# A PV product of 64 rows widened to 128 rows in a fused attention and routed-FFN kernel

## The chip, the cores and the metric

The kernel runs on one core of a Trainium2 chip (trn2). The metric is the device time of one execution in microseconds (us). A profiled execution shows what each engine did: PE (TensorE, matmul), PEld (TensorE's weight load), DVE (VectorE), ACT (ScalarE), POOL (GpSimd) and SP (SyncE, which here issues the DMAs). A matmul on PE contracts over the partitions ("rows") of its two operands: the stationary one is loaded first by a weight load, the moving one is streamed through, one column of the result after another.

## The reference

Two batches of 512 tokens with a hidden size of 512 go through an attention layer with 32 query heads and 8 key/value heads of size 128, then a layer norm, then a base FFN with eight sparsemax-routed LoRA experts, and a layer norm again. Only the attention's product with V is touched here.

```python
q = (x @ Wq).reshape(B, S, 32, 128).transpose(0, 2, 1, 3)
k = (x @ Wk).reshape(B, S, 8, 128).transpose(0, 2, 1, 3)      # each repeated for 4 heads
v = (x @ Wv).reshape(B, S, 8, 128).transpose(0, 2, 1, 3)      # each repeated for 4 heads
scores = where(causal, einsum("bhqd,bhkd->bhqk", q, k) * 128**-0.5, -inf)
out = einsum("bhqk,bhkd->bhqd", softmax(scores), v)
x = layernorm(x + out.reshape(B, S, 4096) @ Wo)
x = layernorm(x + base(x) + experts(x))
```

## The kernel before

Every float32 operand is split into two float16 tiles, a high half and a low half, and a product is made of three matmuls: high by high, high by low, low by high (`mm3`, line 225, whose matmuls all carry line 228).

The work is cut into 16 groups, each a pair of a key/value head `g` and a batch `b`, and every group into four units, `i` = 0 to 3, each of 128 query rows of all four heads. `unit_a` makes the scores on PE, masks them and takes their maximum on DVE (line 369), their exponential on ACT (line 374), and writes the probabilities as two float16 halves into the tile `phl` (high half on ACT, line 350; low half on DVE, lines 354 and 356). A DMA transpose, issued by SP (line 99), turns `phl` into `pt`, with the keys on the partitions. `unit_b`, one unit later, multiplies V with `pt` into the PSUM tile `pv` and evicts it as `o` (ACT line 232, DVE line 233). `unit_c`, two units later, multiplies `o` with Wo and adds the result to `acc`.

While the units of one group run, the projections of the next group are made, in the order K and Q0 (unit 0), Q1 (unit 1), V (unit 2), Q2 and Q3 (unit 3). V's projection ends in `end_v`: ACT writes V's high half into the tile `v2`, DVE its low half, and ACT (line 307) fills a third part of `v2` with the first 64 keys of each block of 128, twice over. One DMA transpose then turns the three parts, 12 blocks of 128 by 128, into the tile `vt`, which has two buffers.

The causal mask makes two cases of a unit's 128 query rows, since for the first 64 of them only the first 64 keys of the diagonal block count. For these 64 rows the diagonal block's probabilities sit in `pt` as one block of 128 rows: the high halves for the 64 keys in the upper 64 rows, and the low halves for the same keys in the lower 64. That is why V's high half for those keys is stored twice (`vd`): one product of 128 rows gives high by high and high by low. The third product, V's low half by the high halves of the probabilities, uses 64 rows of both operands.

In `unit_b` a unit has 3`i` full products of 512 columns for the blocks under the diagonal, then two products of 256 columns for the first half of the query rows (`vd`, and the one of 64 rows), then three of 256 columns for the second half: 5, 8, 11 and 14 matmuls for `i` = 0, 1, 2, 3. The one of 64 rows stands after `vd`'s and before the three of the second half, and all others have 128 rows.

A scheduler decides the order of instructions on each engine for most of the kernel. The first stage, which loads the weights of group 0 and takes their scales, and the last stage, the final group and the FFN of four token tiles, have an order written out by hand. In the first stage `end_v(0, 0, PK[5])` stands in line 750, between `x_max` and the parked projection of Q3. SP's queue is in order: a DMA whose data are late holds those behind it. Behind the first `vt` transpose stand four loads of weights of group 1 (`w1raw`), four loads of `acc`, and the first `pt` transposes.

Of the kernel before, what the change touches and what calls it, by code (L numbers as in the profile page):

```python
# [10 lines left out]
F16 = mybir.dt.float16  # L11
# [6 lines left out]
P = 128  # L18
R = P // 2
NB, S, HID = 2, 512, 512  # L20
NT = S // P
# [18 lines left out]
def kernel(  # L40
# [18 lines left out]
    nc = tc.nc  # L59
    const = ctx.enter_context(tc.tile_pool(name="const", bufs=1))  # L60
    sb = ctx.enter_context(tc.tile_pool(name="sb", bufs=1))
# [19 lines left out]
        )  # L81
    cmh = const.tile([P, 1], F32, tag="cmh", name="cmh")
    nc.gpsimd.memset(cmh, -0.5)
    ones = const.tile([P, P], F32, tag="ones", name="ones")
    nc.gpsimd.memset(ones, 1.0)

# [11 lines left out]
    def sync_transpose(dst, src):  # L98
        hist.append(nc.sync.dma_start_transpose(dst, src).ins)
# [125 lines left out]
    def mm3(dst, pairs, first=True, last=True):  # L225
        n = len(pairs)
        for j, (a, b) in enumerate(pairs):
            nc.tensor.matmul(dst, a, b, start=first and j == 0, stop=last and j == n - 1)  # L228

    def cut_psum(hi, lo, psrc, by):  # L230

        nc.scalar.activation(hi, psrc, AF.Copy, scale=by)  # L232
        return nc.vector.scalar_tensor_tensor(lo, psrc, by, hi, ALU.mult, ALU.subtract).ins  # L233

    KT, QT, VT, LM = {}, {}, {}, {}
# [15 lines left out]
    def cut(b, g, j):  # L251
        return CUT if g else CK[b][:, j : j + 1]
# [19 lines left out]
    def pj(name, tag="pj"):  # L272
        return ps.tile([P, S], F32, tag=tag, name=name, bufs={"pj": 2, "S": 4}.get(tag, 1))

    def mul_k(g, b, tag="pj"):
        pk = pj(f"pk{g}_{b}", tag)
        project(pk, g, b, 4)
        return pk

    def end_k(g, b, pk):  # L280
        k2 = sb.tile([P, 2, S], F16, tag="K", name=f"k{g}_{b}", bufs=2)
        cut_psum(k2[:, 0, :], k2[:, 1, :], pk, cut(b, g, 4))
        KT[(g, b)] = k2
# [6 lines left out]
    def end_q(g, b, h, pq):  # L290

        if h % 2 == 0:
            QT[(g, b, h // 2)] = sb.tile([P, 2, 2 * NT, 2, R], F16, tag="Q", name=f"q{g}_{b}_{h}", bufs=NQ)
        q2 = QT[(g, b, h // 2)][:, :, :, h % 2, :]
        return cut_psum(q2[:, 0], q2[:, 1], pq.rearrange("p (j q) -> p j q", q=R), cut(b, g, h))

    def mul_v(g, b, tag="pj"):
        pv = pj(f"pvp{g}_{b}", tag)
        project(pv, g, b, 5)
        return pv  # L300

    def end_v(g, b, pv):
        v2 = sb.tile([P, 3, S], F16, tag="V2", name=f"v2{g}_{b}")
        cut_psum(v2[:, 0, :], v2[:, 1, :], pv, cut(b, g, 5))

        keys = v2[:, 0, :].rearrange("p (t k) -> p t k", k=P)[:, :, :R]
        nc.scalar.copy(
            v2[:, 2, :].rearrange("p (t a k) -> p t a k", a=2, k=R), keys.unsqueeze(2).broadcast_to([P, NT, 2, R])
        )
        vt = sb.tile([P, 3 * NT, P], F16, tag="VT", name=f"vt{g}_{b}", bufs=2)  # L310
        sync_transpose(vt, v2.rearrange("p a s -> p (a s)"))
        VT[(g, b)] = vt

    def proj(g, b, j):
        if j == 4:
            factors(g, b)
            end_k(g, b, mul_k(g, b))
        elif j == 5:
            end_v(g, b, mul_v(g, b))
        else:  # L320
            end_q(g, b, j, mul_q(g, b, j))

# [66 lines left out]
    def unit_b(g, b, i):  # L389
        vt = VT[(g, b)]  # L390
        pt = PT.pop((g, b, i))
        pt = pt.rearrange("p e k (h q) -> p e k h q", q=R)
        pv = ps.tile([P, HPG, 2, R], F32, tag="PV", name=f"pv{g}_{b}_{i}")
        dst = pv.rearrange("p (e h) j q -> p j e h q", e=2)
        m = 2 * i + 1
        pairs = []
        for kt in range(i):
            ph, pl = (pt[:, :, k :: m][:, :, :2].rearrange("p e j h q -> p j e h q") for k in (kt, i + 1 + kt))
            vh, vl = vt[:, kt, :], vt[:, NT + kt, :]
            pairs += [(vh, ph), (vh, pl), (vl, ph)]  # L400
        if i:
            mm3(dst, pairs, last=False)

        vh, vl, vd = (vt[:, k * NT + i, :] for k in range(3))
        both = pt[:, :, i]
        mm3(dst[:, 0], [(vd, both), (vl[:R], both[:R])], i == 0, i == 0)
        ph, pl = pt[:, :, m + i], pt[:, :, m + 2 * i + 1]
        mm3(dst[:, 1], [(vh, ph), (vh, pl), (vl, ph)], i == 0)
        yield
        o2 = sb.tile([P, 2, HPG, 2, R], F16, tag="O", name=f"o{g}_{b}_{i}", bufs=2)  # L410
        cut_psum(o2[:, 0], o2[:, 1], pv, 2.0**-15)
        OT[(g, b, i)] = o2
        yield
# [269 lines left out]
    with tc.manual_schedule(engines={ET.PE, ET.DVE, ET.Activation, ET.Pool, ET.SP}):  # L683
        for c in range(KC):
            nc.sync.dma_start(x_raw[0][c], xt[0, :, c, :])
            if c == 0:
                load_w(4)
        for j in JS[1:]:
            load_w(j)
        for c in range(KC):  # L690
            nc.sync.dma_start(x_raw[1][c], xt[1, :, c, :])
        wo_raw = [load_raw(source(0, j), f"0_{j}", True) for j in ROWS]
        x0_raw = [load_raw(xt[0, :, c, :], f"x0_{c}") for c in range(KC)]
        w1_raw = [load_raw(source(1, j), f"1_{j}") for j in JS[:2]]
        load_x(0)

        sq0 = sb.tile([P, 8], F32, tag="sq", name="sq0", bufs=2)
        sq1 = sb.tile([P, 8], F32, tag="sq", name="sq1", bufs=2)
        PK[4] = pj("park4", "pj")
        for c in range(KC):  # L700
            x_hi(0, c)
            x_lo(0, c, nc.vector)
            if c < 2:
                n = slice(0, 1) if c == 0 else slice(1, KC)
                hi, lo = (a[:, n, :].rearrange("p c d -> p (c d)") for a in WR[4])
                raw = w_raw[4][:, n.start * P : n.stop * P]
                nc.scalar.copy(hi, raw)
                nc.vector.tensor_tensor(lo, raw, f(hi), ALU.subtract)
            project(PK[4], 0, 0, 4, [c])
        w_hi(0, nc.scalar.copy)  # L710
        w_lo(0, nc.vector)
        park(0, "pj")
        w_hi(1, nc.scalar.copy)
        w_lo(1, nc.gpsimd)
        park(1, "PV")
        w_hi(5, nc.scalar.copy)
        w_hi(2, nc.scalar.copy)
        w_lo(2, nc.gpsimd)
        w_hi(3, nc.scalar.copy)
        w_lo(3, nc.gpsimd)  # L720
        for c in range(KC):
            x_max(0, c)
        w_max(4)
        w_max(5)
        amax(mx[:, 6:7], mx[:, 9:13])
        for j in range(4):
            w_squares(sq0[:, j : j + 1], w_raw[j], "S")
        nc.scalar.activation(sq0[:, 4:7], mx[:, 4:7], AF.Square)
        w_lo(5, nc.vector)
        tot = total(sq0, 7, "0", "S")  # L730
        park(5, "wo")
        for c in (0, 1):
            x_hi(1, c)
            x_lo(1, c, nc.gpsimd)
        sc = sb.tile([P, 2, 8], F32, tag="sc0", name="sc0")
        SC[(0, False)] = sc
        scales(sc, tot, 7)
        x_factors(0, sc, 6)
        end_k(0, 0, PK[4])
        end_q(0, 0, 0, PK[0])  # L740
        factors(0, 0)
        end_q(0, 0, 1, PK[1])
        for c in (2, 3):
            x_hi(1, c)
            x_lo(1, c, nc.gpsimd)
        park(2, "S")
        for c in range(KC):
            x_max(1, c)
        amax(mx[:, 7:8], mx[:, 13:17])
        end_v(0, 0, PK[5])  # L750
        park(3, "S")
        for k in range(4):
            w_squares(mx[:, 17 + k : 18 + k], wo_raw[k], "S")
        amax(sq1[:, 1:2], mx[:, 17:21])
        nc.scalar.activation(sq1[:, 0:1], mx[:, 7:8], AF.Square)
        end_q(0, 0, 2, PK[2])
        tot = total(sq1, 2, "1")
        convert = split_x(0, x0_raw)
        next(convert)
        end_q(0, 0, 3, PK[3])  # L760
        sc1 = sb.tile([P, 2, 8], F32, tag="sc1", name="sc1")
        scales(sc1, tot, 2)
        SC[(0, True)] = sc1[:, :, 1:3]
        x_factors(1, sc1, 0)
        next(convert)

        w1 = sb.tile([P, KC, S], F32, tag="base0", name="w1raw")
        for n, j in enumerate(JS[2:]):
            w1_raw.append(w1[:, n, :])
            sync_load(w1[:, n, :].rearrange("p (c d) -> p c d", c=KC), source(1, j))  # L770
        load_x(1)
# [94 lines left out]
    for s in range(len(units) - NT):  # L866
        if s < len(units):
            g, b, i = units[s]
            k = s // NT
# [80 lines left out]
```

## Time and profile before

| | |
|---|---|
| time, median of 3 runs | 686.54 us (685.78 to 686.63) |
| the profiled execution's own time | 685.9 us |
| its span, first to last instruction | 684.1 us |
| PE busy | 669.8 us, 98% of the span |
| DVE busy | 534.1 us, 78% |
| ACT busy | 362.6 us, 53% |
| POOL busy | 244.2 us, 36% |
| granted PE clock, mean over the span | 0.997 |
| matmuls that write `pv` | 608, of which 64 have 64 rows |
| `vt` transposes | 16, median 1.62 us of SP each, 3.9 us to landing |
| `pt` transposes | 128, median 1.29 us of SP each, 3.6 us to landing |

A group in the profile is a set of instructions with one line, engine, operation and shape. Its "mean ns of one" is the time from an instruction's start to its end. Matmuls are pipelined, one starting before the last has ended, so what a matmul costs the engine is the distance from its start to the next one's start, which the timeline gives, and not its own duration. "128\*128 128x256" is a stationary operand of 128 rows by 128 columns and a moving one of 128 rows by 256 columns; "64\*128 64x256" has 64 rows in both.

### The profile page before, as it was taken

The page shows a single profiled execution, that of the slowest core. Times are in us where ns is not written, and L with a number is a line of the kernel's source. Part 1 is how long each engine was busy: PE and PEld are TensorE (multiplying, and loading weights), DVE is VectorE, ACT ScalarE, POOL GpSimd, SP SyncE. Part 2 cuts the span into 40 slices and gives each one's busy share as a digit, 9 for nine tenths or more (in the row PEclk, how much of TensorE's full clock was granted, in tenths as well). Part 3 has the DMA queues.
Part 4 walks back from the last instruction along what each step waited for, and adds up shares of the span by engine and source line. Part 5 has one row for each costly group of instructions (what it writes and reads, how often), then busy time and mean ns, then how long its engine had stood idle before and what let it go on. Part 6 is the DMA issues. An engine that isn't in the chain of part 4 may idle for free.

```text
span 684.1 us, 11487 instructions
## 1 busy us (share of the span) xinstructions
PE 669.8 (98%) x3596; PEld 344.7 (50%) x3596; DVE 534.1 (78%) x1701; ACT 362.6 (53%) x1030; POOL 244.2 (36%) x353
## 2 busy tenths in 40 slices
PE   8899999999999999999999999999999999999996
PEld 5665545445454545455454544454454545544453
DVE  6897877868697678778788787859777677878796
ACT  6875754566365554656355464626555464444520
POOL 4666450725617050645208067054406001100011
PEclk9999999999999999999999999999999999999998
DMA  8767391747447192555528355734625262453311
GB/s 326 238 104 154 90 208 38 156 109 176 72 73 151 29 216 39 128 118 126 128 54 214 76 103 107 179 64 79 145 42 110 40 118 48 87 112 73 70 44 46
DMA packets 197005, 76.80 MB, mean 112 GB/s; under 512 B 181712, under 2 KB 181712, under 8 KB 196944
## 3 DMA queue, kind: packets, MB, share of 16 engines
q1 hardware_dynamic: 196944, 76.07, 49.8%
q8 instruction: 28, 0.46, 0.3%
q14 instruction: 33, 0.27, 0.1%
HBM read 29.12 MB, written 2.10 MB: 46 GB/s over the span
## 4 chain that ended last, share of the span: by engine, by line
PE 87%; DVE 7%; ACT 2%; DMA 2%; issue 1%; POOL 0%; SPq 0%; POOLq 0%; ACTq 0%; DVEq 0%
PE pw L228 22%; PE pq L228 22%; PE pv L228 15%; PE s L228 12%; PE pvp L228 6%; PE pk L228 5%; PE pa L228 3%; PE park L228 1%; DVE phl L354 1%; ACT s L374 1%; DVE s L369 1%; DMA w1raw<-in_wq_dram 1%; DMA xraw<-in_xt_dram 1%; DVE mx L122 1%; DVE acc L434 1%
## 5 line engine op out<-in xcount | busy, mean ns | idle before, releaser
L374 ACT ACTIVATE s<-s,ast 128x192 f32<-128x192 f32 (+7 forms) x256 | 120.8, 472 | 159.9 <-DVE ast L369 156.2
L228 PE MATMUL pw<-w,o 128*128 128x512 f16 x768 | 177.0, 379 | 0.0
L228 PEld LDWEIGHTS <-w 128*128 128x128 f16 x1008 | 98.1, 98 | 110.5
L228 PE MATMUL pq<-xT,w 128*128 128x512 f16 x672 | 152.2, 379 | 0.0
L350 ACT ACTIVATE phl<-s,ast 128x192 f16<-128x192 f32 (+7 forms) x256 | 110.6, 512 | 23.1 <-DVE ast L343 21.0
L228 PE MATMUL pv<-pt,vt 128*128 128x512 f16 (+2 forms) x608 | 121.1, 325 | 0.3 <-DMA pt<-phl 0.3
L369 DVE CUSTOM_DVE_ANT_0 s<-s,mask,lm 128x192 f32<-128x192 f32 (+7 forms) x256 | 117.7, 519 | 0.7 <-PE s L228 0.7
L354 DVE SCALAR_TENSOR_TENSOR phl<-s,ast,phl 128x128 f16<-128x128 f32 (+2 forms) x224 | 112.4, 515 | 6.4 <-ACT phl L350 5.9
L228 PEld LDWEIGHTS <-o 128*128 128x128 f16 x768 | 74.8, 98 | 77.0 <-DVE o L233 0.7
L228 PE MATMUL s<-k,q 128*128 128x320 f16 (+7 forms) x768 | 106.3, 286 | 1.3 <-DVE phl L356 0.9
L228 PEld LDWEIGHTS <-vt 128*128 128x128 f16 (+1 forms) x608 | 53.8, 99 | 67.4 <-issue 21.3
L228 PEld LDWEIGHTS <-q 128*128 128x128 f16 x768 | 64.1, 98 | 43.1 <-issue 1.6
L260 POOL TENSOR_SCALAR lm<-sc,xs 128x1 f32<-128x1 f32 x15 | 4.0, 265 | 213.6 <-DVE sc L136 125.1
L119 POOL TENSOR_TENSOR w<-raw,w 128x512 f16<-128x512 f32 x70 | 79.5, 1155 | 0.3
L434 DVE SCALAR_TENSOR_TENSOR acc<-pw,lm,acc 128x512 f32<-128x512 f32 x64 | 47.8, 746 | 26.1 <-PE pw L228 25.7
L116 POOL TENSOR_SCALAR raw<-raw,sc 128x512 f32<-128x512 f32 x70 | 47.6, 690 | 56.6 <-issue 32.7
L233 DVE SCALAR_TENSOR_TENSOR o<-pv,o 128x512 f16<-128x512 f32 x64 | 43.7, 683 | 26.5 <-ACT o L232 26.5
L232 ACT ACTIVATE o<-pv 128x512 f16<-128x512 f32 x64 | 39.3, 613 | 42.8 <-PE pv L228 42.7
L122 DVE TENSOR_REDUCE mx<-raw 128x1 f32<-128x512 f32 x68 | 44.4, 678 | 14.9 <-DMA raw<-in_wo_dram 14.9
L374 ACT ACTIVATION_READ_ACCUMULATOR s<-s,ast 128x1 f32 x256 | 51.5, 201 | 0.0
L233 DVE SCALAR_TENSOR_TENSOR q<-pq,q 128x512 f16<-128x512 f32 x56 | 38.0, 683 | 15.8 <-ACT q L232 15.4
L232 ACT ACTIVATE q<-pq 128x512 f16<-128x512 f32 x56 | 34.0, 611 | 26.5 <-PE pq L228 26.5
(166 smaller groups left out, 643.0 us busy)
## 6 DMA issues: line engine op xcount, KB each, us to landing
raw<-in_wo_dram SPq DMA_DIRECT2D x32, 256.0 KB, 3.6
raw<-in_wq_dram SPq DMA_DIRECT2D x29, 256.0 KB, 4.2
xraw<-in_xt_dram SPq DMA_DIRECT2D x8, 256.0 KB, 4.9
raw<-in_wk_dram SPq DMA_DIRECT2D x8, 256.0 KB, 3.4
raw_x<-in_xt_dram SPq DMA_DIRECT2D x8, 256.0 KB, 4.6
acc<-in_x_dram SPq DMA_DIRECT2D x8, 256.0 KB, 5.5
pt<-phl SPq DMA_TRANSPOSE x128, 3.6
out_dram<-y SPq DMA_DIRECT2D x8, 256.0 KB, 2.0
```

Source lines behind the costliest of these rows:

```text
L116: nc.gpsimd.tensor_scalar(view, view, by, 1.0, ALU.mult, ALU.mult)
L119: return first.ins, nc.gpsimd.tensor_tensor(lo, view, hi, ALU.subtract).ins
L122: nc.vector.tensor_reduce(dst, view, AX.X, ALU.max, apply_absolute_value=True)
L228: nc.tensor.matmul(dst, a, b, start=first and j == 0, stop=last and j == n - 1)
L232: nc.scalar.activation(hi, psrc, AF.Copy, scale=by)
L233: return nc.vector.scalar_tensor_tensor(lo, psrc, by, hi, ALU.mult, ALU.subtract).ins
L260: engine.tensor_scalar(lm[:, 4:5], sc[:, 0, 4:5], XS[b][0], 1.0, ALU.mult, ALU.mult)
L350: nc.scalar.activation(hi, src[:, :n], AF.Copy, scale=by)
L354: nc.vector.scalar_tensor_tensor(lo, src[:, :m], by, hi[:, :m], ALU.mult, ALU.subtract)
L369: nc.vector.tensor_tensor_reduce(out=sc[:, :n], in0=sc[:, :n], in1=mask[:, S - n :], scale=lm[:, h // 2 : h // 2 + 1], scalar=BIG, op0=ALU ...
L374: nc.scalar.activation(sc[:, :n], sc[:, :n], AF.Exp, bias=st[:, 0, h : h + 1], scale=-1.0, accum_out=st[:, 1, h : h + 1])
L434: nc.vector.scalar_tensor_tensor(a, pw, LM[(g, b)][:, 7:8], a, ALU.mult, ALU.add)
```

## The change

The product of 64 rows becomes one of 128. `v2` gets a fourth part, one block of 128 keys for each block of the sequence: its first 64 keys are V's low half, its other 64 are zero. After the transpose this is the block `vz`, of 128 rows, and `both` is used whole: its lower 64 rows meet zeros. Since the zeros have to be written only once, `v2` is no longer taken from a pool for every group but is one tile that stays in place; GpSimd clears its fourth part at the start.

For every group ACT makes one more copy, of 4 by 64 elements per partition, and it reads what DVE writes as V's low half. The transpose has 16 blocks instead of 12, and `vt` 16 instead of 12. The copies and the transpose move into a function of their own, `turn_v`, which the ordinary groups call right after `end_v`. In the hand-written first stage it is called later than `end_v`: after `next(convert)`, which issues the split of two of the four tiles of x, and ahead of `end_q(0, 0, 3, ...)`.

```diff
     cmh = const.tile([P, 1], F32, tag="cmh", name="cmh")
     nc.gpsimd.memset(cmh, -0.5)
+    v2 = const.tile([P, 4, S], F16, tag="v2", name="v2")
+    nc.gpsimd.memset(v2[:, 3, :], 0.0)
...
     def end_v(g, b, pv):
-        v2 = sb.tile([P, 3, S], F16, tag="V2", name=f"v2{g}_{b}")
         cut_psum(v2[:, 0, :], v2[:, 1, :], pv, cut(b, g, 5))
 
-        keys = v2[:, 0, :].rearrange("p (t k) -> p t k", k=P)[:, :, :R]
+    def turn_v(g, b):
+
+        first, twice = (v2[:, k : k + 2, :].rearrange("p a (t k) -> p a t k", k=P) for k in (0, 2))
         nc.scalar.copy(
-            v2[:, 2, :].rearrange("p (t a k) -> p t a k", a=2, k=R), keys.unsqueeze(2).broadcast_to([P, NT, 2, R])
+            twice[:, 0].rearrange("p t (a k) -> p t a k", a=2), first[:, 0, :, :R].unsqueeze(2).broadcast_to([P, NT, 2, R])
         )
-        vt = sb.tile([P, 3 * NT, P], F16, tag="VT", name=f"vt{g}_{b}", bufs=2)
+        nc.scalar.copy(twice[:, 1, :, :R], first[:, 1, :, :R])
+        vt = sb.tile([P, 4 * NT, P], F16, tag="VT", name=f"vt{g}_{b}", bufs=2)
         sync_transpose(vt, v2.rearrange("p a s -> p (a s)"))
         VT[(g, b)] = vt
...
             end_v(g, b, mul_v(g, b))
+            turn_v(g, b)
...
-        vh, vl, vd = (vt[:, k * NT + i, :] for k in range(3))
+        vh, vl, vd, vz = (vt[:, k * NT + i, :] for k in range(4))
         both = pt[:, :, i]
-        mm3(dst[:, 0], [(vd, both), (vl[:R], both[:R])], i == 0, i == 0)
+        mm3(dst[:, 0], [(vd, both), (vz, both)], i == 0, i == 0)
...
         convert = split_x(0, x0_raw)
         next(convert)
+        turn_v(0, 0)
         end_q(0, 0, 3, PK[3])
```

## The prediction

> **What bounds the kernel now.** I read the busy shares and the chain of waits first.
>
> ```profile
> PE 669.8 (98%) x3596; PEld 344.7 (50%) x3596; DVE 534.1 (78%) x1701; ACT 362.6 (53%) x1030; POOL 244.2 (36%) x353
> ...
> PE 87%; DVE 7%; ACT 2%; DMA 2%; issue 1%; POOL 0%; SPq 0%; POOLq 0%; ACTq 0%; DVEq 0%
> ```
>
> PE is busy for 98% of the span and is 87% of the chain that ends last. By stages (the windows view), PE is busy 100.00 us of every 100 from 100 to 500 us. The idle time is in the first 45 us and after 598 us. In between, whatever shortens PE's stream shortens the kernel, if the other engines keep up. A busy PE can still hide stalls between overlapping matmuls, so I go to the timeline, for the smallest PV unit (`i` = 0, 5 matmuls) and the scores ahead of it:
>
> ```profile
> 303.57 1.31 PE L228 MATMUL s<-k,q 128*128 128x192 f16 x12
> 304.72 2.75 PE L228 MATMUL pq<-xT,w 128*128 128x512 f16 x12
> ...
> 307.31 0.27 PE L228 MATMUL pv<-pt,vt 128*128 128x256 f16 x1
> ...
> 307.51 0.28 PE L228 MATMUL pv<-pt,vt 64*128 64x256 f16 x1
> ...
> 307.73 0.50 PE L228 MATMUL pv<-pt,vt 128*128 128x256 f16 x3
> 308.06 0.28 PE L127 MATMUL totl<-fsq,ones 128*128 128x1 f32 x2
> ```
>
> Columns are start, length, engine, operation. Go from start to start. Six score matmuls of 192 columns and six of 256 take 304.72 - 303.57 = 1.15 us for 2,688 columns, so 256 columns cost 0.11 us; the three after 307.73 also take 0.33, 0.11 each. But the matmul before the one of 64 rows holds PE for 0.20 us, and the one of 64 rows for 0.22: 0.42 where two of 128 rows would take 0.22. The loss is **0.20 us per unit**. The longer units agree:
>
> ```profile
> 249.27 2.05 PE pv L228 x11
> ...
> 257.01 2.59 PE pq L228 x12
> 259.60 2.70 PE pv L228 x14
> ```
>
> Twelve of 512 columns take 2.59, 0.216 each. Fourteen PV matmuls are nine of these and five of 0.109: 2.49, against 2.70. Eleven are six and five: 1.84, against 2.05. The excess is 0.21 both times. The weight loads say why:
>
> ```profile
> L228 PEld LDWEIGHTS <-vt 128*128 128x128 f16 x544 | 47.8, 99 | 47.6 <-issue 1.8
> L228 PEld LDWEIGHTS <-vt 64*128 64x128 f16 x64 | 5.9, 93 | 19.8 <-issue 19.6
> ```
>
> The 64 small loads sit 19.6 us, 0.31 each, waiting for nothing that is visible, while the 544 full ones have 1.8 in all: the small load isn't pulled under the running matmul.
>
> **The matmul, rule against row.** The Trainium skill, "TensorE: Matmul & The Clock Gate", section "LDWEIGHTS (loading the stationary operand)", says a load's time goes by its columns and a 32-row load takes as long as a 128-row one. By that rule the change gains nothing, and the durations seem to agree: 93 against 99 ns for the loads, 280 against 275 ns for the matmuls. The same skill's "TensorEngine Tiling", section "Key Properties", says a change of tiling mode drains the array, and 64 by 128 is listed there as a mode of its own. Two changes per unit at the drain that the first page gives under "Step-by-step: what each phase is for" (about 128 cycles, 53 ns at 2.4 GHz) would be an estimate of 0.11 us per unit. The trace has 0.20, and the trace decides: the sum for 59 units is 0, 6.3 or 11.8 us by the three. After the change every matmul of the unit has the shape of its neighbours, whose distance is 0.11.
>
> How many of the 64 lie on the path? In the chain in order of time PE carries it without a break from 45 us to 598.36, when it goes to ACT and DVE (`o`, the routing of a token tile, scores). From there to 648.9 its longer pieces touch PE only at 610.5 and 623.7 to 627.8, in other matmuls. The units at 614, 622, 634, 644 and 658 us are off it, the one at 650.2 is on it. So 58 + 1 units: 59 x 0.199 (0.42 - 0.22, unrounded) = **11.7 us**; all 64 would be 12.7, the upper end.
>
> **ACT's second copy.** The copy it joins (512 elements) takes 0.64 us. The exponent-to-half cuts of line 350 take 0.695 at 512 and 0.493 at 256 elements, so half the size saves about 0.20: 0.44 us, 16 times, 7 us of an engine that is busy 53%. It also waits for DVE's low half, with the exponentials of the next unit queued behind it. In the groups from 85 us on the present copy ends within 0.44 us of the low half's end (161.53 against 161.63 us, for instance). Behind it:
>
> ```profile
> 160.92 0.61 ACT L307 COPY v<-v 128x512 f16<-128x512 f16 x1
> 164.61 0.61 ACT L374 ACTIVATE s<-s,ast 128x448 f32<-128x448 f32 x1 [3.07 <-DVE ast L369]
> ```
>
> ACT then idles 3.07 us for DVE's maximum; the groups to 560 us have 2.3 to 3.1. (In the second group, at 42.6, the low half is 1.9 behind and ACT has no idle time; there the new order puts the second copy behind four exponentials, at the low half's end.) Wait and copy are at most 0.9, so they cost nothing. Without that cover, the exponentials, `phl` and `pt` of unit 3 would be late.
>
> **The transpose.** 16 blocks for 12: SP's 1.62 us becomes at most 4/3 of it, 2.2, and 3.9 to landing at most 5.2 (estimates in proportion). Landings of `vt` come 21 to 27 us before the first PV in all groups but the first, so its own lateness is nothing. What follows in SP's queue is `pt` of unit 2 or 3 and weight loads; their `pt` lands 1.2 us or more before its PV from 64 us on. 0 to 0.5 us late costs nothing.
>
> **`v2` in place.** V's next high half is written long after the transpose has landed (at 41.3 us against about 32.5 in the first group, some 30 us later in the others), and the same wait existed with one pool buffer. Clearing the fourth part is one POOL fill at 2.3 us, where POOL has nothing until 9.45. Nothing.
>
> **The first group.** Here `turn_v` moves past four squares, Q2's cut and two x splits on ACT, and the transpose with it on SP:
>
> ```profile
> 24.63 1.54 SPq L99 DMA_TRANSPOSE vt<-v  x1
> 26.27 0.82 SPq L96 DMA_DIRECT2D w1raw<-in_wq_dram  x1
> ...
> 29.44 1.80 SPq L96 DMA_DIRECT2D acc<-in_x_dram  x4
> 32.68 1.19 SPq L99 DMA_TRANSPOSE pt<-phl  x1
> ```
>
> On ACT the squares come 0.6 earlier, but then wait for DVE's maximum as now (23.91); the splits end at 25.94, the two copies at about 26.9. The transpose issues there, 2.3 later than now, so `w1raw`, `acc` and the first `pt` follow 2.3 to 2.9 later: `pt` at about 34, 1 to 1.4 late, since SP had 1.4 us in hand. Q3's cut and what is behind it on ACT slips 0.9. Against this stands what the scheduler's new order shows: DVE no longer waits 0.91 us for `w1raw` ahead of K's cut, for which PE now idles 0.82, and seven more V-projection matmuls (1.6 us) are put ahead of the first PV on PE. `vt` lands near 32.5, PV starts at 37.4. Bounds: 0.8 gained to 2.4 lost. I take 0, near the middle of the two listed effects; both ends stay in the range.
>
> **Sum.** 685.9 of the profiled execution less 11.7 is 674.2 (span 684.1 to 672.4). The median of the runs is 0.64 above that execution: 686.54 - 11.7 = **674.8 us**.
>
> **Rivals.**
> 1. *The others can't follow (half the gain).* DVE is busy 77 to 79 of 100 us in the middle; with PE 1.8% shorter that is 79 to 81. `pt` has its least margin in the unit at 482 us (1.2) and 493 (1.5), against 0.2 us taken per unit; DVE's work is fed by PE's scores and moves with them. For it: three units after 440 us have under 1.6. If half is lost: 680.7.
> 2. *Nothing changes.* If the stall belongs to reading that block of `vt` or `pt`, and not to the 64 rows, it stays: 686.5. Against it: `vd` reads the same `pt` block just ahead without a late load.
> 3. *Slower, through ACT's wait.* Place: the second copy waits in ACT's order for V's low half; should DVE put that half late, unit 3's exponentials stand behind it in 14 groups. Cover is 1.9 us (2.3 idle less 0.44) and unit 3's `pt` margin, 3.05 in the mean (1.3 to 5.0). The change ends slower than before once the wait is over 1.9 + 3.05 + 11.7/14 = 5.8 us per group. At 7: 674.8 + 14 x (7 - 4.95) = 703.5. The trace has 0.44 or less in steady groups, 3.3 once in the first.
>
> **Chances.** Forecast, with at least three quarters of the gain: 0.86. Half: 0.08. Nothing: 0.03. Slower: 0.03. Differences under 0.2% (1.4 us) can't be told from none here. Faster 0.94, same 0.03, slower 0.03. The range goes from 686.5 - 12.7 - 0.8 = 673.0 up to the loss of a fourth of the gain, 677.8, which also holds the first group's worst case (677.2).
>
> **What would show it.** Right: no `64*128` shape; five matmuls of unit 0 in about 0.55 us instead of 0.75; PV of 14 in 2.50; the `issue` idle of `vt`'s loads near 1.8 us in all; the steady period of a group, from one V projection to the next, shorter by 0.8 us (four units). First group: the first PV at 37 to 39 us. Tail, from the last group's first PV to the end, unchanged within 1 us. Wrong: starts still 0.2 apart at `vz`, PE idle for `pt` behind ACT copies that wait on DVE, or a first PV past 40 us.

## The result, and the profile after

The changed kernel takes 677.42 us (677.06 to 678.01, 4 runs) against 686.53 us beside it (685.78 to 686.63, 4 runs): a ratio of 0.9871, interval 0.9853 to 0.9888. The gain is 9.1 us. The forecast was 674.8, a gain of 11.7, so 2.6 us are missing. The time is inside the range that was given, 673.0 to 677.8.

| | before | after |
|---|---|---|
| profiled execution's span | 684.1 us | 675.4 us |
| PE busy | 669.8 us | 658.4 us |
| granted PE clock, mean | 0.997 | 0.997 |
| PE's share of the chain that ended last | 87% | 77% |
| DVE's share of that chain | 7% | 12% |
| `vt` transposes: SP's time, time to landing | 1.62, 3.9 us | 2.3, 4.6 us |

PE's busy time fell by 11.4 us, the span by 8.7. The page of the kernel after has the busy shares, the chain, and the weight loads of V that answer to the two groups of before:

```profile
PE 658.4 (97%) x3596; PEld 350.5 (52%) x3596; DVE 532.3 (79%) x1701; ACT 367.8 (54%) x1046; POOL 244.7 (36%) x354
...
PE 77%; DVE 12%; DMA 3%; ACT 3%; issue 2%; POOL 1%; POOLq 0%; SPq 0%; DVEq 0%; ACTq 0%
...
L230 PEld LDWEIGHTS <-vt 128*128 128x128 f16 x608 | 59.0, 99 | 49.4 <-issue 1.7
```

All 608 loads now have 128 rows, and the 19.6 us of "issue" idle ahead of the 64 small ones are gone; 1.7 is left for all. The timeline of PE (start, length, engine, operation) shows the smallest unit and the stretch in which something else goes wrong:

```profile
283.27 2.00 PE L230 MATMUL pv<-pt,vt 128*128 128x512 f16 x11
285.11 2.75 PE L230 MATMUL pw<-w,o 128*128 128x512 f16 x12
287.70 0.42 PE L230 MATMUL s<-k,q 128*128 128x64 f16 x6
288.66 0.22 PE L230 MATMUL s<-k,q 128*128 128x64 f16 x2 [0.55 <-DVE phl L361]
289.92 0.37 PE L230 MATMUL s<-k,q 128*128 128x64 f16 x4 [1.04 <-DVE q L235]
...
295.31 2.65 PE L230 MATMUL pv<-pt,vt 128*128 128x512 f16 x14
297.80 2.54 PE L230 MATMUL pw<-w,o 128*128 128x512 f16 x11
...
304.13 0.71 PE L230 MATMUL pv<-pt,vt 128*128 128x256 f16 x5
304.67 0.28 PE L129 MATMUL totl<-fsq,ones 128*128 128x1 f32 x2
```

Five PV matmuls take 304.67 - 304.13 = 0.54 us, start to start, instead of 0.75; eleven take 285.11 - 283.27 = 1.84 instead of 2.05; fourteen take 2.49 instead of 2.70. At 288 us, though, PE stands still twice, 1.59 us in all, for DVE. The kernel before had no idle time of PE over 50 ns between 60 and 560 us.

**Where the gain goes.** I laid the start of each PV unit in the trace of after against the same unit of before. Each unit should bring the next one forward by 0.21 us. This is what the traces show, in us:

| PV unit | at (before) | after | only the matmul changed | full gain would be |
|---|---|---|---|---|
| 3 | 64.43 | -0.13 | -0.53 | -0.63 |
| 12 | 151.10 | -1.73 | -2.35 | -2.51 |
| 26 | 287.93 | -4.66 | -4.97 | -5.43 |
| 27 | 298.28 | -2.97 | -3.52 | -5.64 |
| 46 | 482.43 | -6.75 | -7.26 | -9.61 |
| 47 | 492.81 | -6.56 | -6.78 | -9.82 |
| 58 | 609.18 | -8.71 | -8.95 | -12.1 |
| end | 684.11 | -8.71 | -8.97 | -12.3 |

Between these places each unit gains its 0.209. The losses of after are 0.50 by unit 3, 0.29 ahead of unit 5, 1.90 at unit 27, 0.10 at unit 38, 0.40 at unit 47, 0.15 at unit 57 and 0.21 at the end (the unit at 650 us gains nothing): 3.55. And 59 x 0.209 = 12.33, less 3.55, is 8.78, against 8.71 in the trace. The fourth column is an experiment below: a kernel without the new transpose shows nearly the same losses.

**What PE waits for at 288 us.** The view of waits from 280 to 300 us, kernel after (engine, line, awaited, us in total, times, longest):

```profile
DVE mx L124 <- DMA raw<-in_wo_dram: 5.1, 1, 5.1
...
PE s L230 <- DVE q L235: 1.0, 1, 1.0
...
PE s L230 <- DVE phl L361: 0.5, 1, 0.5
```

The long wait is not PE's but DVE's: for the rows of Wo of the next head, whose maximum it has to take. DVE's timeline shows who stands behind it:

```profile
279.27 0.16 DVE L348 SCALAR_TENSOR_TENSOR ast<-ast,s 128x2 f32<-128x2 f32 x1
284.51 0.69 DVE L124 TENSOR_REDUCE mx<-raw 128x1 f32<-128x512 f32 x1 [5.08 <-DMA raw<-in_wo_dram]
...
285.70 0.28 DVE L361 SCALAR_TENSOR_TENSOR phl<-s,ast,phl 128x64 f16<-128x64 f32 x1
...
286.62 0.69 DVE L235 SCALAR_TENSOR_TENSOR q<-pq,q 128x512 f16<-128x512 f32 x1
...
289.18 0.68 DVE L235 SCALAR_TENSOR_TENSOR q<-pq,q 128x512 f16<-128x512 f32 x1
```

DVE works in its queue's order. The maximum of a weight that nobody needs for tens of microseconds stands ahead of `phl` and of the two low halves of `q` of the next group, and PE's scores wait for the second of them, at 289.92. SP's timeline, first of the kernel after, then of the kernel before, gives one reason why the rows are late:

```profile
276.61 2.33 SPq L101 DMA_TRANSPOSE vt<-v  x1
278.99 4.32 SPq L98 DMA_DIRECT2D raw<-in_wo_dram  x4
```

```profile
281.10 1.66 SPq L99 DMA_TRANSPOSE vt<-v  x1
282.81 2.30 SPq L96 DMA_DIRECT2D raw<-in_wo_dram  x4
```

The loads are queued behind V's transpose, and it takes SP 2.33 us instead of 1.66. Counted back from the start of PV unit 26 in each trace (283.27 and 287.93), the loads are issued 4.28 us ahead of it instead of 5.12. That is the smaller part of the delay: the first rows then land 5.5 us after their issue instead of 3.25 (the last section comes back to this). DVE waited for these rows in before too, and it cost PE nothing; the waits of DVE from 60 to 560 us, before and then after:

```profile
DVE mx L122 <- DMA raw<-in_wo_dram: 14.9, 12, 2.5
```

```profile
DVE mx L124 <- DMA raw<-in_wo_dram: 19.7, 9, 5.1
```

How much room was there? These are DVE's second `q` of that stretch and the four scores that read it, in the trace of before:

```profile
292.16 0.67 DVE L233 SCALAR_TENSOR_TENSOR q<-pq,q 128x512 f16<-128x512 f32 x1
```

```profile
292.89 0.37 PE L228 MATMUL s<-k,q 128*128 128x64 f16 x4
```

`q` ends at 292.83, and the scores start 0.06 us later. Under the stall in after the distance is the same: `q` ends at 289.86, the scores start at 289.92. So at this head the kernel before had no room at all, although its waits show nothing, and none at the last one, near 482 us; at the heads whose Wo is loaded near 130, 209 and 364 us its `q` was 0.4 to 0.7 us early.

From the start of unit 26, the second `q` ends after 4.90 us in before and after 6.59 in after: 1.69 later. The faster PV unit lets PE ask for it 0.21 earlier. Together that is 1.90, the loss at unit 27. Only 0.21 of it is PE's own speed.

So three things can have cost the 2.6 us: the longer transpose; a faster PE that meets a wait of DVE's that was always there; or rows of Wo that land late for another reason.

### The profile page after: what moved, and what is told of

The parts are those of the page before. It is cut to its first block, busy times and chain, and to the rows that moved or that the text cites. A ratio compares the mean times of both kernels' runs of the same rounds, so it can differ in the third digit from the quotient of the medians.

```text
span 675.4 us, 11498 instructions
## 1 busy us (share of the span) xinstructions
PE 658.4 (97%) x3596; PEld 350.5 (52%) x3596; DVE 532.3 (79%) x1701; ACT 367.8 (54%) x1046; POOL 244.7 (36%) x354
## 4 chain that ended last, share of the span: by engine, by line
PE 77%; DVE 12%; DMA 3%; ACT 3%; issue 2%; POOL 1%; POOLq 0%; SPq 0%; DVEq 0%; ACTq 0%
PE pw L230 20%; PE pq L230 19%; PE pv L230 12%; PE s L230 11%; PE pk L230 5%; PE pvp L230 5%; PE pa L230 3%; DVE phl L359 2%; ACT s L379 2%; DVE s L374 2%; PE park L230 1%; DMA raw<-in_wo_dram 1%; DVE mx L124 1%; DMA pt<-phl 1%; DVE q L235 1%
## 5 line engine op out<-in xcount | busy, mean ns | idle before, releaser
L230 PE MATMUL pv<-pt,vt 128*128 128x256 f16 (+1 forms) x608 | 107.7, 323 | 0.6 <-DMA pt<-phl 0.3
L230 PEld LDWEIGHTS <-vt 128*128 128x128 f16 x608 | 59.0, 99 | 49.4 <-issue 1.7
```

## The experiments

All but the last two were timed in rounds, beside runs of the kernel before on the same chip (medians 686.40 for the first four, 686.37 for the others, 686.38 for the last).

| run | us (lowest to highest, runs) | ratio to before |
|---|---|---|
| only_matmul | 676.18 (674.9 to 678.15, 4) | 0.9849 (0.9832 to 0.9866) |
| only_v2 | 686.45 (685.06 to 688.82, 14) | 1.0001 (0.9991 to 1.001) |
| turn_early | 681.85 (679.38 to 683.4, 6) | 0.9923 (0.9905 to 0.9941) |
| loads_early | 678.02 (677.44 to 679.47, 4) | 0.9876 (0.9863 to 0.989) |
| matmul_loads | 674.92 (674.5 to 675.02, 5) | 0.9828 (0.9814 to 0.9841) |
| after_loads | 675.12 (674.18 to 676.01, 4) | 0.9831 (0.9818 to 0.9845) |
| before_loads | 686.19 (685.73 to 686.99, 13) | 0.9996 (0.9988 to 1.0004) |
| rows96 | 676.94 (1) | |
| twice64 | 692.42 (1) | |

### The matmul alone, and the rest alone

only_matmul, an edit of before:

```diff
-        mm3(dst[:, 0], [(vd, both), (vl[:R], both[:R])], i == 0, i == 0)
+        mm3(dst[:, 0], [(vd, both), (vl, both)], i == 0, i == 0)
```

> Kernel before with one edit: the product of 64 rows takes vl and both whole, 128 rows; V keeps three parts, one copy, and a transpose of 12 blocks. (It adds V's low half of the block's other 64 keys times the low halves of the probabilities, so its output isn't the reference's.) The order on PE, DVE and SP is that of before. My theory: the matmul alone is worth the forecast 11.7 us, and the missing 2.6 went to the longer transpose and the moved first group: 674.8 (674.3 to 675.4), no PE idle between 60 and 560 us. Rival: a faster PE runs into the pace of the others, and the matmul alone is worth only 9 us: 677.4, with PE idle in the middle.

only_v2, an edit of after:

```diff
-        mm3(dst[:, 0], [(vd, both), (vz, both)], i == 0, i == 0)
+        mm3(dst[:, 0], [(vd, both), (vz[:R], both[:R])], i == 0, i == 0)
```

> Changed kernel with the product put back to 64 rows of the zeroed block (same result), so four parts, two copies, 16 blocks and the moved first group remain, and the order on every engine is that of the changed kernel. My theory: the longer transpose delays the loads of Wo behind it, DVE waits for them, and the first group loses 0.5: 687 to 689 us, since a slower PE leaves DVE some more room than in the changed kernel. Rival: these parts are free, 686.5.

My theory was that the matmul alone brings the full 11.7 and that the longer transpose eats the rest. The matmul alone, with the transpose of before, gives 676.18, and in its profiled execution it loses nearly as much as the changed kernel. Its PE timeline:

```profile
287.39 0.42 PE L228 MATMUL s<-k,q 128*128 128x64 f16 x6
288.11 0.22 PE L228 MATMUL s<-k,q 128*128 128x64 f16 x2 [0.30 <-DVE phl L356]
289.37 0.37 PE L228 MATMUL s<-k,q 128*128 128x64 f16 x4 [1.04 <-DVE q L233]
```

It is the same stall at the same place, with 1.34 us of idle time for 1.59. There DVE waits 2.26 and 1.89 us for the rows of Wo, where it waited 2.00 and 0.70 in before. (Three smaller stalls, at 212, 366 and 481 us, are 0.14, 0.07 and 0.57.) The rest alone costs nothing that 14 runs can tell from none (1.0001), though single executions spread over 3.8 us; its profiled one, at 688.02, has 0.54 lost by unit 3 and 1.56 at the same stall, with PE as slow as in before. By the medians the matmul alone misses 1.5 of the 11.7 us (686.40 - 676.18 is 10.2) and the changed kernel 2.6; their intervals overlap, so how much of the difference is the transpose's isn't settled by these two. So the longer transpose isn't needed for the loss, and neither is the faster PE for the stall. Counted from the start of unit 26 as above, the second `q` ends 6.35 us after it in only_matmul and 6.47 in only_v2, for 4.90 in before: 1.45 and 1.57 later, nearly all of the 1.66 and 1.56 that the two profiled executions lose at this place. In only_matmul the second load of Wo lands later by that much, with the transpose as short as before. The rival, that a faster PE meets an unchanged wait, thus accounts for 0.2 us at the large stall; it fits better at 481 us, where there was no room either and DVE's wait (2.47) is no longer than in before (2.54): PE is idle for 0.57 us there.

### The loads of Wo ahead of the transpose

The plan of before and after names the unit in which a step of `prepare(g, ROWS)` is issued; the first step issues the four loads. loads_early moves it two units ahead, for every head from 2 on:

```diff
-            at(prepare(g, ROWS), u - 1, u, u + 1, u + 2, u + 2, u + 3, u + 3)
+            at(prepare(g, ROWS), u - 3, u, u + 1, u + 2, u + 2, u + 3, u + 3)
```

> Changed kernel with the loads of Wo's rows for the next head issued two units earlier, ahead of V's transpose in SP's queue. My theory: DVE's five waits for raw of Wo (2.9 to 5.1 us each) go, and with them PE's idle time at 288 to 290 and at 481 us (1.9 us): 675.5. Rival, that the loads are not what stalls DVE or PE: 677.4 as the changed kernel, with PE idle at the same places.

The result, 678.02, was no gain. The stall at 288 us is gone all the same: unit 27 stands at -5.18. New ones came: at 403 us the loads of another head now fell behind V's transpose and a `pt`. The waits of loads_early from 393 to 406 us:

```profile
DVE mx L124 <- DMA raw<-in_wo_dram: 1.9, 1, 1.9
...
PE s L230 <- DVE phl L361: 0.8, 1, 0.8
```

The PV units fall back by 1.6 us there (unit 38 at -7.38, unit 39 at -6.02, and 0.21 more was due) and by 1.2 at 476, for a `pt` behind a transpose of V. I kept the move for heads 2 to 5 (`g` under 6), among them the one whose stall it cured, and made it in three kernels, the one with only the matmul, the changed one and the one before:

```diff
-            at(prepare(g, ROWS), u - 1, u, u + 1, u + 2, u + 2, u + 3, u + 3)
+            at(prepare(g, ROWS), u - (3 if g < NG - 2 else 1), u, u + 1, u + 2, u + 2, u + 3, u + 3)
```

> only_matmul with the loads of Wo's rows issued two units earlier for heads 2 to 5, ahead of V's transpose. The order on PE is that of before. (Output as in only_matmul.) My theory: the Wo loads, not the width of the transpose alone, are what a faster PE runs into, so PE's idle time at 288 to 290, 212 and 366 us (1.5 us) goes, at 481 us it stays, and the time is 675.0. Rival: the idle time comes from something else in DVE's order and stays or moves: 676.2 as only_matmul.

> Changed kernel with the same earlier loads for heads 2 to 5 only; order on PE as in the changed kernel. My theory: the 1.6 us of PE idle at 288 to 290 us go and, unlike in loads_early, nothing new comes at 403 and 476 us: 675.6. Rival: new waits take their place: 677.4.

> Kernel before with the same earlier loads and nothing else. My theory: PE has no idle time in the middle there, so DVE's shorter waits buy nothing: 686.4. Rival: the loads cost time of their own, with or without the wider product, and the earlier issue gains 1 to 2 us here too: 685.

With the loads out of the way the forecast's gain is there: 674.92 and 675.12, gains of 11.45 and 11.25 against the 11.7 forecast. For after_loads and the changed kernel, which give the reference's output, the intervals of the ratios (0.9818 to 0.9845, 0.9853 to 0.9888) lie apart. The PE timeline of matmul_loads at the place of the stall:

```profile
287.23 0.67 PE L228 MATMUL s<-k,q 128*128 128x64 f16 x12
287.74 2.75 PE L228 MATMUL pk<-xT,w 128*128 128x512 f16 x12
```

Twelve score matmuls run through in 0.51 us. The waits of DVE from 60 to 560 us, in matmul_loads and then in after_loads:

```profile
DVE mx L122 <- DMA raw<-in_wo_dram: 8.8, 10, 2.3
```

```profile
DVE mx L124 <- DMA raw<-in_wo_dram: 9.9, 13, 2.5
```

In after_loads PE has no idle time over 50 ns between 55 and 580 us. The same move in the kernel before changes nothing (0.9996): there PE stood still for none of these waits. So it is shown that the place of the loads costs the changed kernel about 2 us (gains of 9.1 and 11.25) and the kernel before nothing. It isn't shown that PE's speed alone makes the difference: at the large stall the rows themselves landed later, and only_v2 stalls there with a slow PE. With the loads moved, the longer transpose makes no difference that these runs can tell (675.12 against 674.92). after_loads is the version to keep.

### The place of the transpose in the first stage

turn_early puts `turn_v(0, 0)` back to where the work stood before, right behind `end_v`:

```diff
         end_v(0, 0, PK[5])
+        turn_v(0, 0)
...
         next(convert)
-        turn_v(0, 0)
```

> Changed kernel with turn_v(0, 0) called right after end_v(0, 0, PK[5]), as the copy and the transpose were before. My theory: the 0.5 us that the start lost come back, 676.9 us, and w1raw is issued at about 26.7 us and not 29.1. Rival: ACT's second copy then waits for V's low half (24.6 us) ahead of four squares and holds up the start by about 2 us: 679.

It is worse than both theories had it, 681.85. ACT's timeline in turn_early:

```profile
21.05 0.62 ACT L310 COPY v<-v 128x512 f16<-128x512 f16 x1
25.08 0.40 ACT L313 COPY v<-v 128x256 f16<-128x256 f16 x1 [3.41 <-DVE v L235]
25.39 0.60 ACT L686 ACTIVATE junk<-raw 128x512 f32<-128x512 f32 x1
```

The second copy waits 3.41 us for V's low half, and the squares behind it wait with it. PE's timeline has the end of that chain:

```profile
27.38 0.25 PE L230 MATMUL s<-k,q 128*128 128x64 f16 x3 [3.58 <-ACT junk L686]
```

PE is idle 3.58 us, and the first twelve PV units start 4.1 to 6.4 us later than in the kernel before. The later place in the changed kernel is therefore needed: there both copies stand behind the squares and two of the x splits, and ACT doesn't wait for V's low half.

### What the 0.21 us belong to

rows96 gives the third product 96 rows, and twice64 makes the product of 64 rows twice in a row; both are edits of before:

```diff
-        mm3(dst[:, 0], [(vd, both), (vl[:R], both[:R])], i == 0, i == 0)
+        mm3(dst[:, 0], [(vd, both), (vl[:96], both[:96])], i == 0, i == 0)
```

> Kernel before with 96 rows of vl and both in place of 64 (it adds V's low half of 32 other keys times low halves of the probabilities). If what costs 0.20 us a unit is that fewer than 128 rows are used, five matmuls of unit 0 still take 0.75 us from start to start of what follows. If it is the change of the array's tiling, and 96 rows are no tiling of their own, they take 0.55, as with 128 rows, and the time falls by 9 to 12 us.

```diff
-        mm3(dst[:, 0], [(vd, both), (vl[:R], both[:R])], i == 0, i == 0)
+        mm3(dst[:, 0], [(vd, both), (vl[:R], both[:R]), (vl[:R], both[:R])], i == 0, i == 0)
```

> The kernel before with the product of 64 rows made twice in a row (the low half of V is counted twice for the first half of the query rows, so this term of the output is doubled). It asks what the 0.209 us belong to. If they belong to the change between 128 and 64 rows, there are still only two changes per unit: the starts lie about 0.205, 0.11, 0.212 and 0.12 us apart, six PV matmuls of unit 0 take about 0.86 us instead of 0.75, and the time grows by 0.11 us for each of the 59 units on the path, 6.5 us, to about 693. Rival: they belong to each product of 64 rows. Then every one adds about 0.2 and its own 0.11: the starts lie 0.205, 0.21, 0.21 and 0.12 apart, six matmuls take 0.96, and the time grows by about 12.5 us, to 699.

PE's timeline in rows96, and the timeline and the groups of weight loads (a second view) in twice64:

```profile
303.46 0.71 PE L228 MATMUL pv<-pt,vt 128*128 128x256 f16 x5
304.01 0.28 PE L127 MATMUL totl<-fsq,ones 128*128 128x1 f32 x2
```

```profile
309.97 1.03 PE L228 MATMUL pv<-pt,vt 128*128 128x256 f16 x6
310.83 0.28 PE L127 MATMUL totl<-fsq,ones 128*128 128x1 f32 x2
```

```profile
L228 PEld LDWEIGHTS <-vt 128*128 128x128 f16 x544 | 47.7, 99 | 54.3 <-issue 16.3
...
L228 PEld LDWEIGHTS <-vt 64*128 64x128 f16 x128 | 7.1, 94 | 19.8 <-issue 19.6
```

Five matmuls with one of 96 rows take 0.55 us (five of 128 rows take 0.54 in after). Six with two of 64 rows take 0.86. The times, one run each, are where this puts them: rows96 gains 9.4 us (9 to 12 expected), twice64 loses 6.0 (6.5 expected). From one matmul's start to the next, in ns, the median over the 16 or 17 units of `i` = 0 that stand by themselves on PE:

| kernel | `vd` | third product | its repeat | the next three |
|---|---|---|---|---|
| before | 205 | 212 | | 120, 109, 109 |
| twice64 | 205 | 120 | 201 | 119, 109, 109 |
| rows96 | 109 | 113 | | 112, 108, 108 |
| after | 109 | 109 | | 109, 109, 109 |

The second product of 64 rows follows the first at 120 ns. There are now 128 small loads, and they stand idle as long as the 64 did, 19.6 us. So the cost belongs to the change between 128 and 64 rows, about 0.1 us into it and 0.1 us out of it, and neither to each small product nor to a block that isn't full: 96 rows cost nothing.

## Why the forecast was right, and where it was short

**The matmul: right.** 0.20 us per unit was forecast from one unit. The slope over all units is 0.209, and 12.33 for 59 of them where 11.7 stood. This term decided between gain and none: the rule that a load's rows don't count would have said none, and the row was right. The other rule cited, the Trainium skill's "TensorEngine Tiling (Array Packing)", section "Key Properties", on a change of tiling mode, fits what the runs showed: the cost comes at the change, and twice64 has two changes per unit whatever the number of small products. That the array drains there is the page's word; no trace shows it. Its size, estimated there at 0.11 per unit, was short by half; 0.10 + 0.10 was measured.

**The sum: short by 2.6 us, and by luck not by more.** The slope was 0.6 us better than forecast; against the 12.33 it makes, 3.6 us are lost in the profiled execution, 1.90 of them at the one stall. The sum carried PE's whole saving to the end, and the step that failed is the one on the queue behind the transpose: "What follows in SP's queue is `pt` of unit 2 or 3 and weight loads", then "0 to 0.5 us late costs nothing". For `pt` that was tested against its slack and held. The weight loads were named and not followed further. Who waits for them is DVE, in queue order, ahead of `phl` and of the next group's `q`; PE waits for those. There even a small delay isn't free: in the trace of before the second `q` at 292.83 was just in time. The loss is there without the longer transpose too (only_matmul), so the sentence ahead of it, "In between, whatever shortens PE's stream shortens the kernel, if the other engines keep up", needed the same look: at DVE's waits of 2.0 to 2.5 us, once per head, which were in the trace of before, and at the room that PE had behind each. Why the rows landed as late as they did stays open.

**Rival 1, the others can't follow: right in part.** It was priced at half the gain and looked for in DVE's busy share and in `pt`'s margin. What happened is above all one DMA wait in DVE's queue, which made DVE late with `q`; all that is missing is about a fifth of the gain.

**ACT's second copy: right.** It takes 0.41 us in the first group of after and 0.46 in a late group of loads_early (0.44 was estimated), and PE waits for ACT nowhere between 60 and 560 us. Rival 3 has its place and its mechanism: turn_early shows it, 3.4 us of wait, but in the one group where the changed kernel avoids it.

**The transpose's own size.** SP's time was bounded by 2.2 us and is 2.3 in the median (1.8 to 2.8); landing 4.6 is under the bound of 5.2.

**The first group.** `vt` was to issue at 26.9 and does at 27.0; it lands at 31.4 (32.5 forecast). PE's timeline of after has the first PV at 38.99, inside the 37 to 39 named and behind ten matmuls of the next V projection (three in before). It is 1.63 us later than before, and of that 0.50 is left at unit 3. Zero was taken inside bounds of -0.8 to +2.4; in timed runs (only_v2) this cost isn't seen.

**The rest.** No shape of 64 rows is left. The group's period is shorter by 4 x 0.209 = 0.84 us outside the stalls (0.8 forecast). From unit 58 to the end nothing changes (1 us was allowed). Rival 2, no change, is out.

## What to carry to other kernels

A product with fewer rows among full ones isn't cheap: if it drops from 128 to 64 rows, it costs the change in and the change out, about 0.2 us here, and filling it up to 128 rows costs PE less than leaving it small (whoever fills with zeros has them to move: here a longer transpose). Of several small products in a row only the first and the last pay (twice64 had two). Before the saving of the bounding engine is carried to the end, list the waits that it now covers on the engines that feed it, each with its length, with what is queued behind it in order, and with the time from the end of that work to its use: a wait that costs nothing today may have no room left. A load that nobody needs soon can go ahead of a long transpose in its queue, but each place has to be tried: moved for four heads it gained, moved for all it did not. Putting its first reader behind the work that the bounding engine waits for is the other way; it wasn't tried here.

## What was not expected of the hardware

The loads of Wo took longer to land in the changed kernel than their later issue explains. The DMA views of after from 276 to 287 us and of before from 280 to 291 us (queue: packets, MB, share of 16 engines; issue: count, KB, median us to landing):

```profile
q8 instruction: 1, 0.02, 1.3%
...
raw<-in_wo_dram SPq DMA_DIRECT2D x4, 256.0 KB, 5.5
```

```profile
q8 instruction: 1, 0.02, 0.5%
...
raw<-in_wo_dram SPq DMA_DIRECT2D x4, 256.0 KB, 4.6
```

In both a packet of 16 KB that fetches instructions falls into the stretch. In after it starts at 280.63 us, between the loads, and lasts 2.31 us; in only_matmul 1.69 us, at 280.68. In before it starts at 287.06, after the first rows had landed at 286.07, and lasts 0.96 us, near the 0.9 to 1.3 of most others. The first rows landed 3.25 us after their issue in before and 5.5 in after. In only_v2 it lasts 2.42 us, from 285.59. In all these traces it starts 2.3 to 2.9 us ahead of unit 26, in before 0.9. In only_matmul the first rows still landed after 3.3 us and the second only after 4.9 (3.8 in before). That the fetch holds the loads up fits these traces, but no run moved the fetch by itself: it is an inference, and how the 5.1 us of DVE's wait divide between the fetch and the longer transpose stays open.
